# Layer 2's scans with every engine's queue in the order of the source: preparations in a PSUM bank of their own, one bank for the sums

## The chip, the cores and the metric

The kernel runs on one core of a Trainium2 chip. The metric is the device time of one execution in microseconds (us); each kernel's number is the median of several runs. A core has five engines with a queue each: TensorE (PE in the profile, its weight loads PEld), VectorE (DVE), ScalarE (ACT), GpSimd (POOL), and SyncE (SP), which here only issues DMA transfers. Matmuls write into PSUM[...]; everything else lies in SBUF or in DRAM.

## What is computed

Two layers of a vision state-space model on a 64 x 64 image with 96 channels. Each layer normalises its input, projects it to 192 channels and a gate z, runs a 3 x 3 depthwise convolution and a SiLU, scans the result along four directions, normalises the sum of the scans, multiplies with SiLU(z), projects back to 96 channels and adds the input. The change lies in layer 2's scans, cut here to what matters:

```python
xs = jnp.stack([xf, xf[:, :, ::-1], xf[:, :, o1], xf[:, :, o2]], axis=1)   # 4 directions, L = 4096
x_dbl = jnp.einsum('bkdl,kcd->bkcl', xs, x_proj_weight)                    # dt (6), B (16), C (16)
dts = jnp.einsum('bkrl,kdr->bkdl', x_dbl[:, :, :DT_RANK], dt_projs_weight)
delta = jax.nn.softplus(delta + delta_bias[None, :, :, None])
def step(h, t):
    u_t, d_t, B_t, C_t = t
    h = h * jnp.exp(d_t[..., None] * A[None]) + (d_t * u_t)[..., None] * B_t[:, :, None, :]
    y = jnp.einsum('bkdn,bkn->bkd', h, C_t)
    return (h, y)
```

o1 and o2 are snake orders through the rows of the image, one from the top and one from the bottom. The recurrence runs over 4096 positions for 192 channels x 16 states x 4 directions.

## The kernel before, in words

The work of `scans` (line 631) is cut into chunks and units. A chunk is one of two orders p (rows, snake), one of two directions d, and one quarter c of the image: 16 chunks (`GROUPS`, line 509). The 192 channels of the two directions of an order lie in three blocks T of 128 partitions, and the 16 states are taken two at a time (8 values of m), so a chunk has 3 x 8 = 24 units and the whole has 384. A unit works on a tile of 128 partitions x 1024 positions: 64 channels for each of two states.

What a unit j does, by function:

- `fetch_c(j)` (line 785): two DMA transfers of 256 KB from SyncE's queue put the two rows of C, each repeated over 64 partitions, into `cb` (4 buffers).
- `stage_B(j)` (790): two bf16 matmuls repeat two rows of B over the partitions, into the PSUM tile `B` (two banks, one buffer).
- `stage_a(j)` (799): ScalarE takes a = exp(dt x A) into the PSUM tile `m` (two banks, 2 buffers); VectorE takes b = B x du into SBUF (2 buffers).
- `stage_s(j)` (811): VectorE's scan h = a h + b over the 1024 positions (`h` has 4 buffers); ScalarE copies the last column to `carry` for the next chunk (not in the last chunk of a direction).
- `stage_c(j)` (824): GpSimd takes hc = h x C (5 buffers).
- `stage_r(j)` (828): TensorE adds the products of the two states onto the PSUM tile `y` (a fold: two fp32 matmuls, which the profile shows as four passes). At m = 0 it first loads the old sum by matmuls with the identity (line 837); after m = 7 ScalarE copies the sum back (847). `y` has 2 buffers of one bank.

A chunk also needs a preparation, `prelude` (667): `copies` (snake chunks only, 682), `project` (x_dbl of the chunk by 6 fp32 matmuls, 689, and a copy to `xd`, 693), `rows` (C to DRAM, B to bf16, 697 and 699), `residual` twice (the parts of B that bf16 loses, 707, 710, 717), and for each block T a `delta` with five steps: `begin` (matmuls 726, Abs and Relu 740, 741), `logarithm` (four ScalarE activations, 747 to 750), `lost` and `whole` (two GpSimd operations each, 753, 754, 757, 758) and `double` (eight DMA transfers that copy dt and dt x u to both halves of the partitions, line 240). All PSUM results of the preparation use `spare` (649), which takes one of the two buffers of `m`, those of the exponentials. So the 8 banks are: B two, m four, y two.

The loop at line 854 writes the program: at step j it emits `fetch_c(j+2)`, `stage_B(j+1)`, the matmul part of the preparation that is due, `stage_a(j+1)`, then the preparation's ScalarE part (`todo`), `stage_s(j)`, `stage_c(j-1)` and `stage_r(j-5)`. The due steps of the next chunk's preparation within the 24 units stand in two lists at lines 770 to 778: 5 copies, 6 project, 8 rows, 9 and 11 residuals, 13 to 23 the deltas of blocks 0 and 1; the delta of block 2 at 0, 1, 4, 5, 7 of the chunk itself.

This source order is not the order in which the engines get their instructions. The framework orders each engine's queue when it builds the program, by its own estimates of when operands are ready, and only keeps data dependencies. An instruction stays where the source has it only if it is pinned with `tc.keep_in_program_order`, which puts an ordering edge (no wait) to the instruction traced before it on its engine. Before the change only the loads of activation tables are pinned (line 84). [...]

Of the kernel before, what the change touches and what calls it, by code (L numbers as in the profile page):

```python
# [23 lines left out]
TC = 1024  # L24
# [7 lines left out]
NB = 96  # L32
# [11 lines left out]
def two_ss2d_layers(  # L44
# [586 lines left out]
    def scans(weights):  # L631

        xw, dwb, am = weights
        with ExitStack() as sc:
            pre = sc.enter_context(tc.tile_pool(name="pre", bufs=1))
# [10 lines left out]
            xd = pre.tile([128, TC], F32, name="xd")  # L646
            nc.vector.memset(xd[96:128], 1.0)

            def spare(name):

                return pps.tile([128, TC], F32, tag="m", name=name, bufs=2)

# [14 lines left out]
            def prelude(k):  # L667

                p, d, c = GROUPS[k]
                me = state[k] = {}

                def copies():
                    if p == 0:
                        me["u"] = [u[T][:, HT * c : HT * (c + 1)] for T in range(3)]
                        return
                    me["u"] = []
                    for T in range(3):
                        t = pre.tile([128, HT], F32, tag=f"us{T}", name=f"us{k}_{T}", bufs=2)  # L680
                        for v, f in views(p, u[T], c):
                            nc.scalar.copy(f(t), v)  # L682
                        me["u"].append(t)

                def project():
                    ps = spare(f"pj{k}")[0:NC]
                    for T in range(3):
                        for h, half in enumerate(HALF):
                            nc.tensor.matmul(
                                ps[:, halves[h]], xw[p][half, d, T, :], me["u"][T][half],  # L690
                                start=(T == 0), stop=(T == 2),
                            )
                    return lambda: nc.scalar.copy(xd[0:NC], ps)  # L693

                def rows():
                    me["C"] = dram.tile([NS, TC], F32, tag="C", name=f"C{k}")
                    nc.sync.dma_start(out=me["C"], in_=xd[NC - NS : NC])
                    me["B3"] = pre.tile([NB, TC], BF16, tag="B3", name=f"B3{k}", bufs=2)
                    nc.scalar.copy(me["B3"], xd[0:NB])

                def residual(part):


                    B3 = me["B3"]
                    ps = spare(f"rs{k}_{part}")
                    for s in halves:
                        nc.tensor.matmul(  # L707
                            ps[0:NB, s], ident[0:NB, 0:NB], xd[0:NB, s], start=True, stop=False
                        )
                        nc.tensor.matmul(  # L710
                            ps[0:NB, s], less[:, part, :], B3[:, s], start=False, stop=True
                        )

                    def rest_of_it():
                        for r in range(1 + part, 3):
                            q = slice(32 * r, 32 * r + 32)
                            nc.scalar.copy(B3[q], ps[q])  # L717

                    return rest_of_it

                def delta(T):

                    def begin():
                        ps = spare(f"pd{k}_{T}")[:, 0:HT]
                        for h, half in enumerate(HALF):
                            nc.tensor.matmul(  # L726
                                ps[half], dwb[p][96 : NC + 1, d, T, half],
                                xd[96 : NC + 1, halves[h]], start=True, stop=True,
                            )
# [8 lines left out]

                        def parts_of_v():
                            nc.scalar.activation(me["w", T], ps, AF.Abs)  # L740
                            nc.scalar.activation(me["sp", T], ps, AF.Relu)  # L741

                        return parts_of_v


                    def logarithm():
                        nc.scalar.activation(me["w", T], me["w", T], AF.Exp, scale=-1.0)
                        nc.scalar.activation(me["ln", T], me["w", T], AF.Ln, bias=one)
                        nc.scalar.activation(me["t", T], me["w", T], AF.Identity, bias=one)
                        nc.scalar.activation(me["t", T], me["t", T], AF.Identity, bias=less1)  # L750

                    def lost():
                        nc.gpsimd.tensor_sub(me["w", T], me["w", T], me["t", T])  # L753
                        nc.gpsimd.tensor_add(me["ln", T], me["ln", T], me["w", T])  # L754

                    def whole():
                        nc.gpsimd.tensor_add(me["sp", T], me["sp", T], me["ln", T])  # L757
                        nc.gpsimd.tensor_mul(me["su", T], me["sp", T], me["u"][T])  # L758

                    def double():  # L760
                        for nm, of in (("dt", "sp"), ("du", "su")):
# [4 lines left out]

                    return [begin, logarithm, lost, whole, double]


                early = list(zip((13, 14, 17, 19, 20), delta(0))) + list(  # L770
                    zip((16, 18, 21, 22, 23), delta(1))
                )
                early += [
                    (5, copies), (6, project), (8, rows),
                    (9, lambda: residual(0)), (11, lambda: residual(1)),
                ]
                early.sort(key=lambda at: at[0])
                return early, list(zip((0, 1, 4, 5, 7), delta(2)))

# [10 lines left out]
            def stage_B(j):  # L790
# [3 lines left out]
                for s in halves:  # L794
                    nc.tensor.matmul(  # L795
                        ps[:, s], pick(GROUPS[k][1], m), state[k]["B3"][:, s], start=True, stop=True
                    )

            def stage_a(j):
# [3 lines left out]
                a = pps.tile([128, TC], F32, tag="m", name=f"m{j}", bufs=2)  # L803
                nc.scalar.activation(  # L804
                    a, state[k]["dt", T], AF.Exp, scale=am[p][:, 0, d, T, m : m + 1]
                )
                b = mn.tile([128, TC], F32, tag="b", name=f"b{j}", bufs=2)
                nc.vector.tensor_mul(b, live.pop(("B", j)), state[k]["du", T])  # L808
                live["ab", j] = a, b

            def stage_s(j):
# [4 lines left out]
                first, last = (0, NCH - 1) if d == 0 else (NCH - 1, 0)  # L816
                nc.vector.tensor_tensor_scan(  # L817
                    along(d, h), along(d, a), along(d, b),
                    0.0 if c == first else carry[:, T, m : m + 1], ALU.mult, ALU.add,
                )  # L820
                if c != last:
                    nc.scalar.copy(carry[:, T, m : m + 1], along(d, h)[:, TC - 1 : TC])  # L822

            def stage_c(j):
                hc = live["hc", j] = mn.tile([128, TC], F32, tag="hc", name=f"hc{j}", bufs=LAG)
                nc.gpsimd.tensor_mul(hc, live.pop(("h", j)), live.pop(("C", j)))  # L826

            def stage_r(j):
# [5 lines left out]
                if m == 0:  # L834
                    live["y"] = pps.tile([128, HT], F32, tag="y", name=f"ys{j}", bufs=2)
                    for q, (view, f) in enumerate(views(p, y[T], c)):
                        nc.tensor.matmul(  # L837
                            f(live["y"]), ident, view, start=(q == 0), stop=False
                        )
                ps = live["y"]  # L840
                for h, half in enumerate(HALF):
                    nc.tensor.matmul(  # L842
                        ps[half], fold[:, 0:64], v[:, halves[h]], start=False, stop=(m == NP - 1)
                    )
                if m == NP - 1:
                    for view, f in views(p, y[T], c):
                        nc.scalar.copy(view, f(ps))  # L847

            early, late = prelude(0)
            for _, step in early:  # L850
                (step() or bool)()
            waiting = list(late)
            N = len(units)
            for j in range(-4, N + LAG):
                k, i = divmod(max(j, 0), PER)
                if i == 0 and 0 <= j < N:
# [3 lines left out]
                    else:  # L860
                        late = []
                todo = bool
                for step, at in (
                    (fetch_c, j + 2),
                    (stage_B, j + 1),
                    (None, j),
                    (stage_a, j + 1),
                    (stage_s, j),
                    (stage_c, j - 1),
                    (stage_r, j - LAG),  # L870
                ):
                    if step is None:

                        if j >= 0 and waiting and waiting[0][0] <= i:
                            todo = waiting.pop(0)[1]() or bool
                    elif 0 <= at < N:
                        step(at)
                    if step == stage_a:
                        todo()
                if i == PER - 1 and j < N:  # L880
# [319 lines left out]
```

## Time and profile before

The time is 2156.99 us (median of 3 runs, 2152.57 to 2159.94). The profiled execution:

| | busy us | share of the span of 2156.5 us | instructions |
|---|---|---|---|
| PE | 1354.3 | 63% | 3694 |
| DVE | 1598.7 | 74% | 1108 |
| ACT | 894.0 | 41% | 1395 |
| POOL | 1161.7 | 54% | 634 |

How the lines of the profile are read. A row of the table of groups gives the line in the kernel, the engine, the operation, the tile written <- the tiles read, their shapes and the count; after the first bar the busy time in us and the mean of one in ns; after the second the idle time of the engine just before these instructions, and what ended most of it. A row of the waits gives who waited for whom, then the total in us, how often, and the longest. A row of the timeline gives the start and the duration in us, then the engine and the instructions (several alike are merged, xN), and in brackets the idle time before with its releaser. A row of the windows gives the stretch, its length, then busy us and instructions of PE, PEld, DVE, ACT and POOL, the granted TensorE clock as a share of full speed, the share of DMA engines busy, and GB/s.

### The profile page before, as it was taken

The numbers are of one execution on the slowest core, as the hardware profiler recorded it, in microseconds if no ns is written. First come the engines' busy times: TensorE is split into PE (matmuls) and PEld (weight loads), VectorE is DVE, ScalarE is ACT, GpSimd is POOL, SyncE is SP. The second block draws the span as 40 slices with busy tenths as digits, with TensorE's granted clock in tenths as the row PEclk, the third lists the DMA queues.
The fourth block names the chain that finished last, engine by engine and source line by source line (L and its number), as shares of the span: only waits on it lengthen the run. The fifth ranks groups of instructions, "written<-read, shape, count | busy, mean of one in ns | idle before, by whom it ended". The sixth has DMA issues, their size and how long they took to land. (4 is left out here: it accounts for less than half of the span.)

```text
span 2156.5 us, 14481 instructions
## 1 busy us (share of the span) xinstructions
PE 1354.3 (63%) x3694; PEld 370.7 (17%) x3694; DVE 1598.7 (74%) x1108; ACT 894.0 (41%) x1395; POOL 1161.7 (54%) x634
## 2 busy tenths in 40 slices
PE   6337735756575757565666566767666666666578
PEld 3214201111111111111111111211111111111113
DVE  7755793886877777777777777778686868686895
ACT  3343435534343434344444444434344343434333
POOL 0031005574748484857575757475757666565760
PEclk8556866877666776677767675766676766767658
DMA  4133115482837474646464646565464737282854
GB/s 115 29 85 91 36 58 128 119 205 78 201 92 187 107 175 119 164 119 161 121 159 125 168 119 166 128 151 143 126 168 104 190 86 196 76 201 70 209 142 117
DMA packets 125258, 282.18 MB, mean 131 GB/s; under 512 B 39868, under 2 KB 43260, under 8 KB 125068
## 3 DMA queue, kind: packets, MB, share of 16 engines
q1 hardware_dynamic: 121388, 278.01, 50.9%
q10 hardware_dynamic: 3776, 3.15, 0.7%
q8 instruction: 31, 0.51, 0.1%
q14 instruction: 63, 0.52, 0.1%
HBM read 215.07 MB, written 12.13 MB: 105 GB/s over the span
## 5 line engine op out<-in xcount | busy, mean ns | idle before, releaser
L826 POOL TENSOR_TENSOR hc<-h,cb 128x1024 f32<-128x1024 f32 x384 | 895.0, 2350 | 173.5 <-DVE h L817 145.4
L817 DVE TENSOR_TENSOR_SCAN h<-m,carry,b 128x1024 f32<-128x1024 f32 x288 | 674.3, 2345 | 215.8 <-POOL hc L826 178.7
L842 PE MATMUL ys<-hc,fold 128*64 128x512 f32 x1536 | 599.8, 834 | 336.9 <-POOL hc L826 336.2
L808 DVE TENSOR_TENSOR b<-B,du 128x1024 f32<-128x1024 f32 x384 | 466.7, 1215 | 166.6 <-PE B L795 118.0
L804 ACT ACTIVATE m<-dt,am 128x1024 f32<-128x1024 f32 x384 | 428.1, 1116 | 242.2 <-DVE h L817 235.8
L795 PE MATMUL B<-B,selh 96*128 96x512 bf16 x768 | 310.9, 497 | 271.1 <-DVE b L808 270.6
L753 POOL TENSOR_TENSOR w<-w,t 128x512 f32<-128x512 f32 x48 | 60.7, 1265 | 552.5 <-ACT t L750 454.0
L817 DVE TENSOR_TENSOR_SCAN h<-m,b 128x1024 f32<-128x1024 f32 x96 | 219.1, 2286 | 65.4 <-POOL hc L826 52.3
L822 ACT COPY carry<-h 128x1 f32<-128x1 f32 x288 | 54.3, 188 | 496.8 <-DVE h L817 496.5
L842 PEld LDWEIGHTS ys<-hc,fold 128*64 128x64 f32 x1536 | 109.2, 171 | 618.3 <-POOL hc L826 420.0
L795 PEld LDWEIGHTS <-selh 96*128 96x128 bf16 x768 | 69.5, 105 | 655.7 <-issue 646.5
L981 DVE SCALAR_TENSOR_TENSOR acc<-pad,v,acc 128x1052 f32<-128x1052 f32 x96 | 119.2, 1312 | 0.2
L707 PE MATMUL rs<-xd,ident 96*96 96x512 f32 x128 | 69.3, 624 | 38.5 <-ACT xd L693 26.6
L837 PE MATMUL ys<-y,ident 128*128 128x256 f32 (+1 forms) x144 | 83.8, 698 | 10.8 <-ACT y L847 10.8
L847 ACT COPY y<-ys 128x256 f32<-128x256 f32 (+1 forms) x72 | 29.9, 445 | 141.8 <-PE ys L842 141.5
L726 PE MATMUL pd<-xd,dwb 29*64 29x512 f32 x192 | 65.0, 760 | 3.3 <-ACT sp L741 2.2
L754 POOL TENSOR_TENSOR ln<-ln,w 128x512 f32<-128x512 f32 x48 | 60.6, 1262 | 3.7
L757 POOL TENSOR_TENSOR sp<-sp,ln 128x512 f32<-128x512 f32 x48 | 60.5, 1261 | 2.5
L740 ACT ACTIVATE w<-pd 128x512 f32<-128x512 f32 x48 | 28.6, 597 | 71.6 <-PE pd L726 70.0
L717 ACT CAST B<-rs 32x1024 bf16<-32x1024 f32 x48 | 48.1, 1002 | 14.4 <-PE rs L710 13.8
L682 ACT COPY us<-u 128x256 f32<-128x256 f32 x48 | 16.7, 405 | 71.4 <-POOL su L758 71.4
L837 PEld LDWEIGHTS ys<-y,ident 128*128 128x128 f32 x144 | 33.1, 272 | 74.1 <-ACT y L847 46.4
(162 smaller groups left out, 1065.9 us busy)
## 6 DMA issues: line engine op xcount, KB each, us to landing
cb<-C SPq DMA_DIRECT2D x768, 256.0 KB, 4.1
dt<-sp SPq DMA_DIRECT2D x192, 128.0 KB, 4.5
du<-su SPq DMA_DIRECT2D x192, 128.0 KB, 4.1
szd<-sz SPq DMA_DIRECT2D x24, 256.0 KB, 2.5
szt<-szd SPq DMA_DIRECT2D x24, 256.0 KB, 7.2
xT<-xs SPq DMA_DIRECT2D x8, 384.0 KB
xs<-xT SPq DMA_DIRECT2D x1, 1536.0 KB
xs<-xT SPq DMA_DIRECT2D x8, 192.0 KB
```

The lines of the kernel that those rows point to most:

```text
L707: nc.tensor.matmul(ps[0:NB, s], ident[0:NB, 0:NB], xd[0:NB, s], start=True, stop=False)
L726: nc.tensor.matmul(ps[half], dwb[p][96 : NC + 1, d, T, half], xd[96 : NC + 1, halves[h]], start=True, stop=True,)
L753: nc.gpsimd.tensor_sub(me["w", T], me["w", T], me["t", T])
L754: nc.gpsimd.tensor_add(me["ln", T], me["ln", T], me["w", T])
L795: nc.tensor.matmul(ps[:, s], pick(GROUPS[k][1], m), state[k]["B3"][:, s], start=True, stop=True)
L804: nc.scalar.activation(a, state[k]["dt", T], AF.Exp, scale=am[p][:, 0, d, T, m : m + 1])
L808: nc.vector.tensor_mul(b, live.pop(("B", j)), state[k]["du", T])
L817: nc.vector.tensor_tensor_scan(along(d, h), along(d, a), along(d, b), 0.0 if c == first else carry[:, T, m : m + 1], ALU.mult, ALU.add,)
L826: nc.gpsimd.tensor_mul(hc, live.pop(("h", j)), live.pop(("C", j)))
L837: nc.tensor.matmul(f(live["y"]), ident, view, start=(q == 0), stop=False)
L842: nc.tensor.matmul(ps[half], fold[:, 0:64], v[:, halves[h]], start=False, stop=(m == NP - 1))
L981: nc.vector.scalar_tensor_tensor(acc, src, wk, acc, ALU.mult, ALU.add)
```

## The change

All compute instructions of layer 2's scans, from step 0 of the loop on, are pinned to the order of the source on TensorE, ScalarE, VectorE and GpSimd, by a wrapper around each engine; the DMA queue is not. The order of the source is rewritten so that it can be executed as it stands: in a step, B and the exponential of unit j+1 come first, then the fold of j-5, then the whole of the preparation that is due (matmuls and ScalarE part together, no `todo`), then scan j and product j-1. The preparation is cut finer: each half of `project` and of `residual` is a step of its own with 512 columns. Its PSUM results go into one bank of their own ("v"), and `y` has one buffer instead of two, so that the 8 banks are: B two, m four, y one, v one. `double` is done at the end of `whole`.

```diff
+        class Ordered:
...
+                def issue(*args, **more):
+                    ins = op(*args, **more)
+                    return tc.keep_in_program_order(ins) if pinned else ins
...
+        pe, act, dve, pool = (
+            Ordered(e) for e in (nc.tensor, nc.scalar, nc.vector, nc.gpsimd)
+        )
...
-                return pps.tile([128, TC], F32, tag="m", name=name, bufs=2)
+                return pps.tile([128, HT], F32, tag="v", name=name)
...
-                def project():
-                    ps = spare(f"pj{k}")[0:NC]
+                def project(h):
+                    ps = spare(f"pj{k}_{h}")[0:NC]
                     for T in range(3):
-                        for h, half in enumerate(HALF):
-                            nc.tensor.matmul(
-                                ps[:, halves[h]], xw[p][half, d, T, :], me["u"][T][half],
-                                start=(T == 0), stop=(T == 2),
-                            )
-                    return lambda: nc.scalar.copy(xd[0:NC], ps)
+                        pe.matmul(
+                            ps, xw[p][HALF[h], d, T, :], me["u"][T][HALF[h]],
+                            start=(T == 0), stop=(T == 2),
+                        )
+                    act.copy(xd[0:NC, halves[h]], ps)
...
-                def residual(part):
+                def residual(part, h):
...
-                early = list(zip((13, 14, 17, 19, 20), delta(0))) + list(
-                    zip((16, 18, 21, 22, 23), delta(1))
-                )
-                early += [
-                    (5, copies), (6, project), (8, rows),
-                    (9, lambda: residual(0)), (11, lambda: residual(1)),
-                ]
+                early = [
+                    (5, copies), (6, lambda: project(0)), (7, lambda: project(1)), (8, rows),
+                    (9, lambda: residual(0, 0)), (10, lambda: residual(0, 1)),
+                    (11, lambda: residual(1, 0)), (12, lambda: residual(1, 1)),
+                    *zip((13, 14, 16, 18), delta(0)), *zip((15, 17, 19, 20), delta(1)),
+                ]
...
-                return early, list(zip((0, 1, 4, 5, 7), delta(2)))
+                return early, list(zip((0, 1, 3, 4), delta(2)))
...
-                    live["y"] = pps.tile([128, HT], F32, tag="y", name=f"ys{j}", bufs=2)
+                    live["y"] = pps.tile([128, HT], F32, tag="y", name=f"ys{j}")
...
+                if j == 0:
+                    pinned.append(True)
                 for step, at in (
                     (fetch_c, j + 2),
                     (stage_B, j + 1),
+                    (stage_a, j + 1),
+                    (stage_r, j - LAG),
                     (None, j),
-                    (stage_a, j + 1),
                     (stage_s, j),
                     (stage_c, j - 1),
-                    (stage_r, j - LAG),
                 ):
                     if step is None:
-
                         if j >= 0 and waiting and waiting[0][0] <= i:
-                            todo = waiting.pop(0)[1]() or bool
+                            waiting.pop(0)[1]()
```

## The prediction

> **What bounds the kernel now.** I read the page's table of groups first, then the waits of VectorE alone between 351 and 2106 us, where layer 2's scans run (first scan at 351.26, last one ending at 2105.49 us), then the timeline of one chunk.
>
> The three groups of the table that each of the 384 units pays once:
>
> ```profile
> L826 POOL TENSOR_TENSOR hc<-h,cb 128x1024 f32<-128x1024 f32 x384 | 895.0, 2350 | 173.5 <-DVE h L817 145.4
> L817 DVE TENSOR_TENSOR_SCAN h<-m,carry,b 128x1024 f32<-128x1024 f32 x288 | 674.3, 2345 | 215.8 <-POOL hc L826 178.7
> ...
> L808 DVE TENSOR_TENSOR b<-B,du 128x1024 f32<-128x1024 f32 x384 | 466.7, 1215 | 166.6 <-PE B L795 118.0
> ```
>
> VectorE owes a unit 2.345 + 1.215 = 3.56 us, GpSimd 2.35 us. But the stretch takes 2105.5 - 351.3 = 1754.2 us, that is 4.57 us a unit. VectorE's waits in that window say who holds it:
>
> ```profile
> DVE h L817 <- POOL hc L826: 230.9, 31, 9.3
> DVE b L808 <- PE B L795: 118.0, 74, 4.1
> ```
>
> The scan waits for GpSimd 31 times, two long waits in nearly every chunk. One of them in the timeline, first GpSimd, then VectorE:
>
> ```profile
> 823.46 2.34 POOL L826 TENSOR_TENSOR hc<-h,cb 128x1024 f32<-128x1024 f32 x1 [1.18 <-DVE h L817]
> 844.09 1.26 POOL L753 TENSOR_TENSOR w<-w,t 128x512 f32<-128x512 f32 x1 [18.28 <-ACT t L750]
> ...
> 847.99 2.34 POOL L826 TENSOR_TENSOR hc<-h,cb 128x1024 f32<-128x1024 f32 x1
> ```
>
> ```profile
> 839.93 1.23 DVE L808 TENSOR_TENSOR b<-B,du 128x1024 f32<-128x1024 f32 x1 [0.68 <-PE B L795]
> 850.36 2.29 DVE L817 TENSOR_TENSOR_SCAN h<-m,b 128x1024 f32<-128x1024 f32 x1 [9.20 <-POOL hc L826]
> ```
>
> GpSimd stands idle for 18.28 us because a preparation of the next chunk (L753) lies in its queue ahead of products whose scans (824.58, 828.43, 831.97, 835.85) were done. The four h buffers fill and the scan stops. So the order of the queues sets the time here. Scan to scan, the distances of nearly all chunks show the same steps: 7.7 us at unit 2 to 3, 5.7 at 5, 14.6 at 13, 10.7 at 17, the rest mostly 3.5 to 3.6; a chunk (24 units) takes 110 to 113 us. The end of the last chunk, where no preparation is left, shows the rhythm without them:
>
> ```profile
> 2078.25 1.23 DVE L808 TENSOR_TENSOR b<-B,du 128x1024 f32<-128x1024 f32 x1
> ...
> 2079.39 2.34 DVE L817 TENSOR_TENSOR_SCAN h<-m,carry,b 128x1024 f32<-128x1024 f32 x1
> 2079.53 1.01 PE L795 MATMUL B<-B,selh 96*128 96x512 bf16 x2 [1.53 <-DVE b L808]
> ...
> 2080.47 1.98 PE L842 MATMUL ys<-hc,fold 128*64 128x512 f32 x4
> ...
> 2081.84 1.23 DVE L808 TENSOR_TENSOR b<-B,du 128x1024 f32<-128x1024 f32 x1
> ```
>
> 3.58 us a unit, VectorE never waiting. B is ready at 2080.54 and read at 2081.84, so TensorE has some 1.2 us of slack.
>
> [...] the B pair takes 1.01 or 0.59 us, four fold passes 1.98 or 1.08 us, and the granted clock is 0.70 over the scans. [...] The trace has both forms of a projection:
>
> ```profile
> 820.50 4.68 PE L689 MATMUL pj<-u,xw 64*124 64x512 f32 x12
> 101.65 8.04 PE L294 MATMUL npj<-nus,xw 64*124 64x384 f32 x12
> ```
>
> L689 alternates the row halves: twelve 512-column passes in 4.68 us. L294 uses one half only: twelve shorter passes of 384 columns take 8.04 us.
>
> **The change, part by part.**
>
> Order. Each step now holds, per engine: TensorE B of unit j+1, folds of j-5, then a preparation; ScalarE the exponential of j+1, the preparation, the carry of j; VectorE b of j+1, scan j; GpSimd the preparation, then the product of j-1. Take t as the end of scan j-1, and 3.58 us a step. GpSimd: lost() at step 16 needs the logarithm of step 14, done about t(14) + 1.4 + 2.8, before GpSimd is free. Each of the six pairs costs 2 x 1.26 = 2.5 us, a step leaves 3.58 - 2.35 = 1.23 us over; steps 16, 18, 19, 20 pile up at most 1.3 + 0.1 + 1.3 + 1.3 = 4 us. A product may be late by some 9 us (four h buffers) before scan j+3 waits. In all 24 x 2.35 + 12 x 1.26 = 71.5 us a chunk, below 86. So both long waits go. ScalarE: 45 us busy a chunk by the windows view; its worst step, 1.3 + 2.8 = 4.1 us, is taken up by 3.4 us of slack of the exponential. Carries are needed one chunk later. DMA: 768 x 256 KB and 384 x 128 KB are 252 MB, over some 1.45 ms 174 GB/s; the page has slices of 209 GB/s at 8 tenths. The queue is not pinned, and a fetch has about 12 us from its issue to its use, against 4.1 us to landing. I cost it at nothing.
>
> Banks. One bank "v" for preparations frees the "m" buffers for exponentials (24.2 us of waits for m go); one "y" bank makes the first fold of a block wait for the copy of the block before, which lies a step earlier: nothing.
>
> TensorE is where the new order costs. b of j+1 now stands directly before scan j, so a late B stops VectorE, whereas before b could run two ahead. A plain step at half clock is 2079.53 to 2082.37 (the next weight load) = 2.84 us, at full clock 1.53. Added at half / full: delta 1.97 / 1.07, three per chunk; start of a sum (L837) 2.0 / 1.12, three; a quarter of the residuals about 2.1 / 1.15 (325.06 to 329.38 for two, 834.27 to 836.50 for two), four; half a projection, now on one row half, 6 passes x 0.64 x 512/384 = 5.1 / 2.6, two. All at half clock, less 3.58 and the slack: steps 6 and 7 lose 2 x 4.4; 9 to 12 lose 4 x 1.4 - 0.7; 13 (delta and sum start) 3.2; 15 and small rest 0.6: 17.4 us a chunk. All at full clock: about 0.5. How the clock goes is shown by short stretches in the windows view (PE busy is the first number, PEclk the sixth):
>
> ```profile
> 882.30:885.60 3.30, 3.30 (x9) 0.65 (x10) 2.99 (x2) 0.65 (x1) 3.30 (x2) 0.50 0.94 251
> 885.80:889.00 3.20, 2.38 (x12) 0.68 (x10) 3.10 (x3) 1.21 (x2) 2.73 (x2) 1.00 1.07 243
> 854.00:864.50 10.50, 10.48 (x22) 1.54 (x21) 9.57 (x6) 5.72 (x10) 4.47 (x2) 0.50 0.57 151
> ```
>
> A dense run of folds and B brings the full clock after 3.4 to 7 us (also at 773 and 797, with L837), and steps 5 to 6 are such a run; ten dense us with a delta in them did not. I take 5 us: step 6 0.8, step 7 0.6, one residual step 1.4, one more 1.4, step 15 0.5, rounded up.
>
> Start. The first preparation is serial through one bank: the second half of the projection can begin only after the first copy (about 324.6) and runs cold, +5 us; the residuals in four turns +3. I take +8 (3 to 11).
>
> Sum: 351.3 + 8 before the first scan; VectorE 12 chunks x 85.9 + 4 first chunks (scan 2.29) x 84.7 = 1369; TensorE 15 x 5 = 75; after the last scan 51.0; 0.5 between span and time: 1855 us.
>
> **The rivals.**
> - TensorE stays at half clock. For: the third row above, and L294's 8 us on half the rows, which ran at 0.50 too. Against: the grants named there. 15 x 10 to 17.4 more than none: 1930 to 2041 us.
> - The DMA queue or GpSimd becomes the bound: the copies of dt and du (1 MB per block) meet the fetches of cb at a 25% higher pace, and a fetch comes 3.6 us too late three times a chunk. For: slices at 8 tenths. Against: 12 us of lead. 15 x 11 more: about 2020 us.
> - Slower: pinned queues lock together, folds holding back B until the scan is over. For: folds stand ahead of the preparation, and their products come from a GpSimd that now must do the preparation first; nothing can overtake any more. Against: five units of lag, 18 us. Then a unit is 1.01 + 1.22 + 2.35 + 2 x 0.13 = 4.84 us: 384 x 4.84 + 359 + 51 = 2269 us.
>
> **How the numbers follow.** Main case (0.5 to 10 us lost a chunk) 0.68, half clock 0.17, DMA or GpSimd 0.10, slower 0.05. Low end: 351 + 3 + 1369 + 8 + 51 = 1782, taken as 1785. High end: it must take in part of the second and third case, 13 us lost a chunk and +10 at the start: 351 + 10 + 1369 + 195 + 51 = 1976, taken as 1975. No change would need a sum of losses of 20 us a chunk: 0.02. Slower 0.05, faster 0.93.
>
> **What would show it.** Scan to scan 3.5 to 3.6 us in all steps but 6, 7, 9 to 13; the wait of h for hc near zero; VectorE's remaining wait b for B, some 5 us a chunk; the projection's six passes about 2.6 or 5.1 us. Wrong would be: h still waiting for hc, waits for du or cb, or a chunk above 100 us.

## The result and the profile after

The changed kernel takes 1798.37 us (median of 4 runs, 1794.76 to 1799.91) against 2156.79 us: a ratio of 0.8337, with a 95% interval of 0.8318 to 0.8356. It is faster by 358 us; the forecast was 302 us faster, with 1785 to 1975 us as its range.

In the profile after, every compute instruction of the scans goes through the wrapper and so carries its line, 644; the tiles tell them apart. The table of groups (busy us, mean ns | idle us before, releaser):

```profile
L644 POOL TENSOR_TENSOR hc<-h,cb 128x1024 f32<-128x1024 f32 x384 | 900.6, 2355 | 254.9 <-DVE h L644 236.4
L644 DVE TENSOR_TENSOR_SCAN h<-m,carry,b 128x1024 f32<-128x1024 f32 x288 | 674.1, 2341 | 0.0
...
L644 DVE TENSOR_TENSOR b<-B,du 128x1024 f32<-128x1024 f32 x384 | 470.3, 1225 | 93.4 <-DMA du<-su 39.1
```

None of these operations has become shorter to speak of. What has gone is the idle time in front of the scan: 215.8 us before, 0.0 now (for the 96 scans that start a direction, in a row of their own, 65.4 before and 0.0 now). VectorE no longer waits for GpSimd; GpSimd waits for VectorE. VectorE's waits between the first scan (365.09 us) and the end of the last (1747.18 us) have one row left, where before h waited 230.9 us and b 118.0:

```profile
DVE b L644 <- PE B L644: 17.7, 26, 1.2
```

The place that held GpSimd for 18.28 us before, the preparation of blocks 0 and 1, in the timeline of GpSimd after:

```profile
851.23 2.36 POOL L644 TENSOR_TENSOR hc<-h,cb 128x1024 f32<-128x1024 f32 x1 [1.23 <-DVE h L644]
853.54 1.27 POOL L644 TENSOR_TENSOR w<-w,t 128x512 f32<-128x512 f32 x1
...
868.20 2.36 POOL L644 TENSOR_TENSOR hc<-h,cb 128x1024 f32<-128x1024 f32 x1
870.51 1.26 POOL L644 TENSOR_TENSOR sp<-sp,ln 128x512 f32<-128x512 f32 x1
...
873.07 6.99 POOL L644 TENSOR_TENSOR hc<-h,cb 128x1024 f32<-128x1024 f32 x3
```

Preparations start at once, since their logarithm (ScalarE's part, which GpSimd waited for before) is long done, and products alternate with them. The product that starts at 873.07 belongs to a scan that ended at 869.01: 4.06 us late, and it is the latest one of the chunk; by 880 GpSimd has caught up.

The 358.5 us between the two spans (2156.5 and 1798.0), by stretch: the first scan comes 13.8 us later (365.1 against 351.3); from it to the end of the last scan 1382.1 us pass instead of 1754.2, 372.1 less; what follows is alike (50.8 against 51.0).

### The profile page after: what moved, and what is told of

Same layout as the page of the kernel before. It is cut to its first block, busy times and chain, and to the rows that moved or that the text cites. A ratio compares the mean times of both kernels' runs of the same rounds, so it can differ in the third digit from the quotient of the medians.

```text
span 1798.0 us, 14702 instructions
## 1 busy us (share of the span) xinstructions
PE 1350.7 (75%) x3694; PEld 367.9 (20%) x3694; DVE 1595.2 (89%) x1108; ACT 906.1 (50%) x1459; POOL 1165.1 (65%) x634
## 5 line engine op out<-in xcount | busy, mean ns | idle before, releaser
L644 PE MATMUL ys<-hc,fold 128*64 128x512 f32 x1536 | 559.8, 817 | 4.0 <-POOL hc L644 4.0
L644 PE MATMUL B<-B,selh 96*128 96x512 bf16 x768 | 304.8, 488 | 270.3 <-DVE b L644 269.5
L644 PEld LDWEIGHTS ys<-hc,fold 128*64 128x64 f32 x1536 | 93.1, 166 | 249.5 <-issue 166.6
L644 PE MATMUL pj<-u,xw 64*124 64x512 f32 x96 | 51.0, 667 | 39.2 <-ACT xd L644 25.9
L644 PE MATMUL rs<-xd,ident 96*96 96x512 f32 x128 | 74.0, 661 | 4.0 <-ACT B L644 3.2
L644 PE MATMUL pd<-xd,dwb 29*64 29x512 f32 x192 | 75.2, 872 | 0.9 <-ACT sp L644 0.6
L644 ACT CAST B<-rs 32x512 bf16<-32x512 f32 x96 | 55.3, 576 | 11.0 <-PE rs L644 9.2
L644 ACT COPY xd<-pj 124x512 f32<-124x512 f32 x32 | 18.7, 585 | 73.9 <-PE pj L644 73.9
L644 PE MATMUL pj<-us,xw 64*124 64x512 f32 x96 | 45.4, 606 | 0.0
```

Source lines behind the costliest of these rows:

```text
L644: ins = op(*args, **more)
```

## Experiments: which part of the change does it

The times below are medians; the kernel before took 2157 to 2159 us in each of these comparisons.

**Pins.** The changed kernel with nothing pinned: the line `pinned.append(True)` is left out.

```diff
-                if j == 0:
-                    pinned.append(True)
```

> The changed kernel with nothing pinned: banks, finer preparation and new source order stay, the framework orders the queues. Theory (the order of GpSimd's queue was the cost): the framework again puts GpSimd's part of the preparation ahead of products that are ready, a chunk stays near 105 to 113 us, about 2080 to 2170 us. Rival (the preparation's use of the exponentials' PSUM buffers was the cost, and the bank of its own cures it): below 1850 us.

2305.15 us, a ratio of 1.0695 (1.0664 to 1.0727) to the kernel before: slower than before, and slower than either theory allowed. VectorE's waits in this run:

```profile
DVE h L644 <- POOL hc L644: 285.4, 59, 11.6
DVE b L644 <- PE B L644: 236.3, 78, 8.1
```

So bank, finer steps and new source order bring nothing by themselves; without the pins they cost 146 us. And there are two waits here, not one: b for B is nearly as large as h for hc.

**GpSimd alone pinned.**

```diff
-                    return tc.keep_in_program_order(ins) if pinned else ins
+                    return tc.keep_in_program_order(ins) if pinned and self.engine is nc.gpsimd else ins
```

> The changed kernel with GpSimd alone pinned. Theory (GpSimd's order is the one that matters): both long waits of a chunk are gone, 1800 to 1860 us. Rival (the other queues' orders cost as much, for example folds ahead of B on TensorE): above 1900 us, with VectorE's b waiting for B.

2031.57 us, 0.9402 (0.9355 to 0.9449). The rival holds. The scan no longer waits for GpSimd, but b waits 251.0 us for B. One of the waits in the timelines of TensorE and VectorE:

```profile
588.80 2.02 PE L644 MATMUL rs<-xd,ident 96*96 96x512 f32 x2 [1.25 <-ACT B L644]
...
595.66 0.59 PE L644 MATMUL B<-B,selh 96*128 96x512 bf16 x2
...
596.29 1.23 DVE L644 TENSOR_TENSOR b<-B,du 128x1024 f32<-128x1024 f32 x1 [7.50 <-PE B L644]
```

Residual matmuls (rs) take turns with ScalarE's copies through the one bank, and the framework has put B behind them; VectorE stands still for 7.50 us for a B that takes 0.59.

**All but GpSimd pinned**, the counterpart (`is not nc.gpsimd` in the same line).

> The changed kernel with TensorE, ScalarE and VectorE pinned and GpSimd left to the framework. With GpSimd alone pinned the time was 2032 us, with all pinned 1798 us. Theory (two separate costs: products behind preparations on GpSimd, and B behind preparations on TensorE): GpSimd's mistakes come back, the scan waits for products again, 1850 to 2050 us, and b waits little for B. Rival (the framework's GpSimd order is good as soon as the other queues are fixed): 1798 to 1815 us.

2003.74 us, 0.9288 (0.9274 to 0.9303), as the theory had it, with the other wait alone:

```profile
DVE h L644 <- POOL hc L644: 198.3, 73, 4.1
...
DVE b L644 <- PE B L644: 17.4, 24, 1.1
```

**TensorE and GpSimd pinned**, ScalarE and VectorE not (`self.engine in (nc.tensor, nc.gpsimd)`).

> The changed kernel with TensorE and GpSimd pinned, ScalarE and VectorE left to the framework. GpSimd alone gave 2032 us, all but GpSimd 2004 us, all four 1798 us. Theory (the two queues that hold both preparation and work of the current unit ahead of VectorE are these two; ScalarE has slack, VectorE has only b and scan): 1795 to 1825 us. Rival (ScalarE's order is the third cost, exponentials behind logarithms): above 1850 us, with the scan waiting for m.

1802.09 us, 0.8346 (0.8332 to 0.836), within 4 us of the kernel with all four pinned. VectorE's waits: b for B 21.4 us, h for m 3.9 us. These two queues are nearly the whole of what the pins bring here: both hold work of the current unit, which VectorE waits for, and preparations of the next chunk, which nobody needs yet.

**Pins alone.** The kernel before with its own order, steps and banks, and its four engines pinned (the wrapper, its four names in place of `nc.tensor` and so on, and `pinned.append(True)` at j = 0).

> The kernel before with its own source order, its own banks (preparation in the exponentials' buffers, two sum banks) and the projection on both row halves at once, but all four engines pinned from step 0 of the loop on. Theory (the order is all): 1785 to 1830 us; the first scan starts as before, some 14 us earlier than in the changed kernel, and the steps with a preparation lose 0.2 us or so because the exponential waits for the scan before it. Rival (sharing the buffers costs once the order is fixed): several us in each of some 8 steps of a chunk, above 1950 us.

1935.68 us, 0.8976 (0.8956 to 0.8996): between the two, nearer to the rival. Of the 358 us, the pins alone bring 223. The timeline shows where the rest stays, first TensorE, then VectorE:

```profile
577.41 5.05 PE L644 MATMUL pj<-u,xw 64*124 64x512 f32 x12 [1.25 <-DVE h L644]
...
583.40 0.60 PE L644 MATMUL B<-B,selh 96*128 96x512 bf16 x2
...
584.04 1.23 DVE L644 TENSOR_TENSOR b<-B,du 128x1024 f32<-128x1024 f32 x1 [3.10 <-PE B L644]
```

The projection needs a buffer of the exponentials, which a scan sets free when it ends (h in the brackets); only then can it start, and B stands behind it in TensorE's queue.

**The bank alone undone.** That run also differs in its steps. So the changed kernel, pinned and in its new order, with the preparation in the exponentials' buffers again:

```diff
-                return pps.tile([128, HT], F32, tag="v", name=name)
+                return pps.tile([128, TC], F32, tag="m", name=name, bufs=2)[:, 0:HT]
```

> The changed kernel, pinned and in its new order, but the preparation takes the exponentials' PSUM buffers as before (only the bank of its own is undone; the sums keep one bank). Theory (a preparation matmul then waits in TensorE's queue for the end of the scan that frees its buffer, and B of the next unit stands behind it): each of the nine preparation steps with matmuls loses the preparation, B and 0.4 us, that is 2 to 3.6 us, some 23 us a chunk: 2050 to 2160 us. Rival (the bank matters little under a fixed order, and the 1936 us of pinning alone came from its coarser steps): below 1850 us.

2258.70 us, 1.0464 (1.0437 to 1.0492): slower than the kernel before, and well above the theory's range. A step with a delta, TensorE and then VectorE:

```profile
587.65 1.97 PE L644 MATMUL pd<-xd,dwb 29*64 29x512 f32 x4 [4.24 <-DVE h L644]
...
589.55 1.03 PE L644 MATMUL B<-B,selh 96*128 96x512 bf16 x2
...
590.62 1.22 DVE L644 TENSOR_TENSOR b<-B,du 128x1024 f32<-128x1024 f32 x1 [3.03 <-PE B L644]
```

TensorE waits 4.24 us for the end of the scan; then follow the preparation, B, and b, one after the other. Scan to scan such a step takes 6.5 us instead of 3.6, the two halves of the projection 9.5 to 10 us each. b waits 498.4 us for B in the whole run. With the exponential of j+1 ahead of the preparation, as in the new order, both buffers are held when a preparation needs one. So the new order needs the bank. What the finer steps and the new order are each worth with the bank in place was not run.

## Experiments: the sizes of the steps

**GpSimd's backlog.** Two h buffers instead of four.

> The changed kernel with two h buffers instead of four, so that scan j waits for product j-2. Theory (products are up to 4.1 us late behind the preparations, as the trace of the changed kernel shows at units 17 to 20, and two buffers leave 2.4 us): 1.7 us lost near unit 20 and some tenths near unit 3, about 2 us a chunk, 1820 to 1840 us. Rival (no backlog matters): 1798 us; rival (every scan would wait): above 1950 us.

1831.39 us, 33 us more than with four. The scan of unit 20 and its neighbours, in VectorE's timeline of a chunk:

```profile
878.79 2.35 DVE L644 TENSOR_TENSOR_SCAN h<-m,carry,b 128x1024 f32<-128x1024 f32 x1 [0.24 <-POOL hc L644]
...
883.67 2.35 DVE L644 TENSOR_TENSOR_SCAN h<-m,carry,b 128x1024 f32<-128x1024 f32 x1 [1.20 <-POOL hc L644]
```

With 0.3 us more at unit 4 that is some 2 us in each of the 15 chunks with a preparation, and from the first scan to the end of the last 30.0 us more pass than with four. The 4 us of backlog are real, and the four buffers hide them whole.

**TensorE's slack.** Each delta's matmuls are done twice:

```diff
-                        for h, half in enumerate(HALF):
+                        for h, half in [*enumerate(HALF)] * 2:
```

> The changed kernel with the matmuls of each delta done twice (the same result written again): 1.97 us more on TensorE at half clock or 1.07 at full, in steps 0, 13 and 15. Theory (the slack and the half-clock costs of the prediction hold, and only the clock was better than assumed): steps 0 and 15, at half clock, lose 2.84 + 3.94 - 3.58 - 1.2 = 2.0 us each, step 13, at full clock, nothing: 4 us a chunk, about 1860 us. Rival (TensorE has far more room than the prediction gave it): below 1815 us.

1811.51 us, 13 us more: the rival's side of the line. From the first scan to the end of the last 14.1 us are lost, 13.2 of them in step 0 (0 to 1.6 us a chunk); steps 13 and 15 lose nothing. So the theory fell, in its step 15 above all, which it had at half clock with a loss of 2.0 us. The mean granted clock of the profiled run is 0.765, in the changed kernel 0.736 (means over the span); what clock step 15 had is open. Where step 0 lost most, as in the last chunk (5.2 us instead of 3.6), its loss of 1.6 us is near the 2.0 I had worked out for half clock; by that sum it would fit a slack of 1.6 rather than 1.2 us.

**The start.** The first preparation takes the exponentials' two buffers, which are free then:

```diff
+                if len(state) == 1:
+                    return pps.tile([128, TC], F32, tag="m", name=name, bufs=2)[:, 0:HT]
                 return pps.tile([128, HT], F32, tag="v", name=name)
```

> The changed kernel, only the preparation of the first chunk takes the two buffers of the exponentials instead of the single bank. Theory (the later first scan, 365.1 against 351.3 us, is the one bank being used in turns): the first scan starts near 355 us and the time falls by 8 to 12 us to about 1788 us. Rival (the halves' serial work on TensorE at half clock or the transfers of dt and du set the start): no change, 1796 to 1799 us.

1782.97 us, 15 us less than the changed kernel, which is more than the theory said. The first scan starts at 351.52 us, 13.6 us earlier than in the changed kernel and as early as in the kernel before: the one bank is what the later start costs. (The other 2 us or so lie after the scans, where the profile has 48.0 instead of 50.8 us; nothing was changed there.)

**The projection in four steps of 256 columns** (steps 6 to 9; rows at 10, residuals at 11 to 14, deltas from 15 on), together with the start above.

> The changed kernel with the first preparation in the exponentials' buffers (alone: 1783 us) and the projection in four steps of 256 columns, steps 6 to 9, the rest of the preparation two steps later. Theory (the 0.2 to 1.9 us that each chunk still loses at steps 6 and 7 are the projection's serial passes): these go, 15 x 0.9 = 13 us, about 1770 us. Rival (they come from the clock being granted late, or the later deltas bring the transfers of dt and du too close to their use): 1780 us or more.

1782.22 us: no gain on 1782.97 in sum, but two that cancel. From the first scan to the end of the last it takes 1372.4 us instead of 1381.9, and most chunks now take exactly 24 x 3.585 us; b waits 6.2 us for B instead of 17.5. But the first scan starts at 360.21 us: in the first preparation the four pieces now have to take turns in the two buffers. So the first preparation keeps its two pieces in the next run.

> The first preparation in the exponentials' buffers with the projection in two steps, all later projections in four steps of 256 columns. Theory (two savings that add up: first scan at 351.5 us as with the buffers alone, 1372 us from the first scan to the last as with four steps): 351.5 + 1372.4 + 48 = 1772 us, and 0.5 us for the launch. Rival (the savings overlap): 1780 us or more.

1776.68 us (1774.53 to 1777.26). First scan at 351.46, 1370.5 us to the end of the last: both savings are there. That it is not the 1772 of the theory lies after the scans: that stretch took 53.1 us here instead of 48.0, and why is open.

Then the delta of block 0 is written ahead of the residuals in the first preparation:

```diff
-            for _, step in early:
-                step()
+            for i in (0, 1, 2, 3, 8, 9, 11, 13, 4, 5, 6, 7, 10, 12, 14, 15):
+                early[i][1]()
```

> As the run with both savings, and in the first preparation the delta of block 0 is written ahead of the residuals, since its chain through ScalarE, GpSimd and the transfers is the longest. Theory (the first scan waits for du, 26 us): the first scan comes 3 to 6 us earlier, about 1767 us. Rival (the framework orders this unpinned part by itself, or B's residuals end last): 1772 us.

1765.13 us (1765.05 to 1769.32), a ratio of 0.8178 (0.8165 to 0.8191) to the kernel before. The first scan starts at 345.87 us, 5.6 us earlier. The rest of the 11.5 us gained does not lie in the scans, which take 1371.6 us in the profile (of an execution of 1769.32 us); what it is stays open. This version beats both kernels.

## Why the prediction was right, and where it was off

The main case came about, at its lower end. Its sum, term by term:

- **VectorE, 1369 us: right.** The distance from scan to scan that most steps of a chunk have in the profile after is 3.586 us, 3.525 in the four first chunks of a direction: 12 x 86.06 + 4 x 84.60 = 1371.1, less 2.6 for the b of the first two units, which come before the first scan: 1368.5 us. Outside steps 6 and 7 nothing else sets the pace.
- **GpSimd, ScalarE and the DMA queue at nothing: right.** The backlog was forecast at 4 us and is 4.06 us; the slack of 9 us was not tested at its end, but two buffers with 2.4 us of it lost what the difference says. The DMA share rose from 0.57 to 0.74 in the scans, and no fetch is late for VectorE (GpSimd waits for one nine times, 10.2 us in all). The single sum bank cost nothing either: the loads of the old sum stood idle for 10.8 us before and for 0.0 after.
- **TensorE, 75 us (5 us a chunk): mis-sized, it is 14.** 1382.1 - 1368.5 = 13.6 us in 15 chunks, 0.9 us each. The step that failed is the one that takes two residual steps and step 15 as run at half clock and charges 3.3 us for them; they lose nothing. Nor was the slack of 1.2 us, which the prediction itself reads from the last chunk, taken off there: a single residual step at half clock would lose 1.4 - 1.2 = 0.2 us. The windows of the profile after for chunk 4, steps 7 to 14 and then 15 to 17 (PEclk is the sixth number):

```profile
735.00:762.00 27.00, 22.57 (x73) 5.96 (x73) 24.79 (x15) 16.45 (x28) 16.98 (x8) 1.00 0.64 160
762.00:772.00 10.00, 9.57 (x22) 1.54 (x21) 9.64 (x7) 6.47 (x13) 8.76 (x6) 0.52 0.53 143
```

The full clock comes in step 5 to 6, as forecast (0.57 on average from 728.70 to 732.20 us, 1.00 from there on), and then stays for eight steps, through all residuals and the delta of step 13; in steps 6 to 12 it is 1.00 in all 15 chunks with a preparation. Step 15 is at half clock in this chunk (0.50 from 765.81 to 769.40 us) and takes 3.59 us, its neighbours 3.52; by the prediction's figures it has 2.84 + 1.97 - 3.58 = 1.2 us more work than time, about the slack. Residual steps can cost, but less than 1.4 us each: in chunk 6 of the run with the projection in four steps of 256 columns two of them in a row lost 0.3 and 1.0 us. What is left are the two halves of the projection, in the same chunk, TensorE and then VectorE:

```profile
732.28 2.83 PE L644 MATMUL pj<-u,xw 64*124 64x512 f32 x6
735.05 0.61 PE L644 MATMUL B<-B,selh 96*128 96x512 bf16 x2
736.59 2.83 PE L644 MATMUL pj<-u,xw 64*124 64x512 f32 x6
...
735.69 1.23 DVE L644 TENSOR_TENSOR b<-B,du 128x1024 f32<-128x1024 f32 x1 [1.17 <-PE B L644]
...
740.00 1.22 DVE L644 TENSOR_TENSOR b<-B,du 128x1024 f32<-128x1024 f32 x1 [0.89 <-PE B L644]
```

Six serial passes take 2.83 us at a clock of 1.00 (forecast 2.6 at full clock). In this chunk steps 6 and 7 lose 1.1 and 0.8 us, on average over the 15 chunks 0.3 and 0.6 (forecast 0.8 and 0.6). Spreading the passes over four steps took most of this loss away, which shows that it was theirs.

- **The start, 8 us: mis-sized, it is 13.8.** The mechanism was right: the second half waits for the first copy and runs at a clock of 0.50 (324.44 to 329.92 us), in TensorE's timeline

```profile
324.44 5.48 PE L644 MATMUL pj<-u,xw 64*124 64x512 f32 x6 [25.89 <-ACT xd L644]
...
334.31 2.02 PE L644 MATMUL rs<-xd,ident 96*96 96x512 f32 x2 [1.25 <-ACT B L644]
...
344.35 1.97 PE L644 MATMUL pd<-xd,dwb 29*64 29x512 f32 x4 [0.29 <-ACT B L644]
```

and the residuals take turns with ScalarE's copies. What I left out is that the deltas stand behind them in the same bank. The first delta's matmuls (pd) start at 344.35 us in the change; in the kernel before they started at 333.09:

```profile
333.09 2.29 PE L726 MATMUL pd<-xd,dwb 29*64 29x512 f32 x8
```

That is 11.3 of the 13.8 us. Most of the rest comes from the pinned order: b of unit 1, whose B waits for b of unit 0, now stands ahead of the first scan, which starts 3.5 us after b of unit 0 instead of 1.3.

The two errors have opposite signs: 75 - 14 = 61 us too many, 5.8 too few, hence 1855 against 1798. That VectorE's term is right to 0.5 us is in part luck: it has 3.58 for 3.586 us a unit, and it counts the b of units 0 and 1, which come before the first scan. One sum on the side is wrong: no change would need losses of (2157 - 1780) / 15 = 25 us a chunk, not 20.

**What I had not seen.** I argued the gain from GpSimd's queue, with b for B a smaller matter of the new order's cost. The runs show that with the new source and banks TensorE's queue, left to the framework, costs about as much: GpSimd alone pinned leaves 233 us of the way to 1798, all but GpSimd 205 us. How the two share the loss in the kernel before was not run; there h waited 230.9 us for hc and b 118.0 us for B. And I costed the bank by the 24.2 us of waits for m in the trace before; undone under the pinned order it costs 2258.7 - 1798.4 = 460 us. A wait in the trace of one order does not price a resource in another order. Both were on the side of the main case, so the total did not show it.

Of the rivals, TensorE at half clock is refuted by the windows above (1.00) for the steps that carry the projection and the residuals, the DMA queue by VectorE's waits. The slower one, pinned queues that lock together, did not come about in the change, but it did with the bank undone (1.0464), by a buffer instead of by the folds that I had suspected.

**Queues and row halves.** The argument from the order of the queues rests on single waits: GpSimd stood idle for 18.28 us in the kernel before while products were ready, and with GpSimd alone pinned VectorE stood 7.50 us for a B of 0.59 us behind residual matmuls. Beyond such waits it was the author's assumption. The two halves of the projection, one after the other, take 2 x 2.83 us in the change, at a clock of 1.00; both together, the row halves in turn, took 3.65 us in the kernel before (at 488.09 us), at 0.77.

## What to carry to other kernels

When an engine waits for another that stands idle in front of an instruction nobody needs yet, look at the order of that queue before its speed, and do so for every queue that mixes urgent and early work: here, with the new source, GpSimd's and TensorE's cost some 200 us each, and fixing one leaves the other. Fix the order together with the buffers: in the fixed queue with the bank undone, a delta's matmuls waited 4.24 us for a shared buffer, VectorE then waited 3.03 us for the B behind them, and that run, at 2258.70 us, was slower than the kernel before. A buffer plan that suits the steady state may lengthen the first, serial round, here by 13.6 us; there the other buffers are still free.

## What the runs showed of the hardware

The full TensorE clock, once granted, lasted in the change from 735 to 762 us (1.00), with TensorE busy 22.57 of 27.00 us and serial passes on half of the rows among them. In the trace before it came in one place after 3.40 busy us of folds, a B and the start of a sum (the sixth number is the clock):

```profile
793.50:796.90 3.40, 3.40 (x7) 0.83 (x8) 0.52 (x1) 1.47 (x3) 3.32 (x3) 0.50 0.55 155
797.00:800.30 3.30, 2.23 (x8) 0.31 (x6) 3.17 (x3) 0.36 (x3) 3.30 (x2) 1.00 0.15 61
```

In two other places it stayed at 0.50: through 7.50 busy us of serial passes (102.00 to 109.50 us), and through 10.48 busy us of 10.50 with a delta among them (854.00 to 864.50). So the 3.4 to 7 us that the prediction reads from the trace are not enough in every case. In the last chunk of the change, which has no preparation, the clock was 1.00 from 1685.20 to 1688.80 us and 0.50 from 1697 to 1711 us; between 1687 and 1697 us, where TensorE was busy 5.40 of 10.00 us, it was 0.69 on average. With twice the matmuls in each delta the mean clock of the profiled run was 0.765 instead of 0.736. What grants and ends the full clock was not settled.
